# Layer 3 of a four-layer graph network: targets from node 4992 on summed from layer 0's lists, the others through 16 classes of buckets

## The chip, the cores and the metric

The kernel runs on one NeuronCore of a Trainium2 chip. A core has a matrix engine (TensorE; PE in the profile, with its weight loads shown apart as PEld), a vector engine (VectorE; DVE), a scalar engine (ScalarE; ACT), a general engine (GpSimd; POOL) and a synchronising engine (SyncE; SP) that mostly issues transfers. Sixteen DMA engines move the data. Each engine has its own instruction stream, and semaphores order the streams against each other. The metric is the device time of one execution, in microseconds (us). Ten executions of the kernel before took 8581.14 to 8597.47 us, with a median of 8588.27.

## The reference, cut to what matters

There are N = 12500 nodes of 128 features and E = 200000 edges with a source `src` and a target `dst`. The sources are uniform. The targets are the floor of 12500 times the square of a uniform number, so low node numbers have far more edges than high ones, and the edges come sorted by target. All inputs are drawn from seed 0.

```python
edge_index = stack([src, dst])
h = relu(layernorm(x)); x = x + L0(h)    # attention over the edges into dst
h = relu(layernorm(x)); x = x + L1(h)    # 8 heads, sums into row = src, reads col = dst
h = relu(layernorm(x)); x = x + L2(h)    # sums both ways, weighted by degrees
h = relu(layernorm(x)); x = x + L3(h)    # mean over the edges into dst

def L2(x):
    row, col = concat([src, dst]), concat([dst, src])
    deg = segment_sum(ones, row) + 1;  dinv = rsqrt(deg);  xw = x @ W
    return segment_sum(dinv[row] * dinv[col] * xw[col], row) + dinv**2 * xw + b

def L3(f):
    neigh = segment_sum(f[src], dst) / max(indegree, 1)
    h = f @ W_self.T + neigh @ W_neigh.T + b
    h = (h - mean(h, 0)) * rsqrt(var(h, 0) + eps) * gamma + beta   # over all nodes
    return f + relu(h)
```

## The kernel before

The nodes lie in NB = 98 blocks of P = 128, so NP = 12544 with padding. The edges lie in tiles of 128. Sums over edges are made in two ways.

**By lists and gathers.** For a tile of 128 edges a list in SBUF holds the row numbers to read, and one indirect DMA of POOL (`gather`, line 292) brings these 128 rows of a table in DRAM. A matrix of ones and zeros ("hot"), made by DVE by comparing each edge's place with a row of numbers, sums the rows into the nodes of a block by a matmul, and DVE adds the result to an accumulator in SBUF. Layer 0 works on windows of G = 4 tiles of the edges as they come, sorted by target. There are NW = 391 windows, and a window touches two blocks of targets at most; otherwise the flag `sparse`, which `windows` (line 935) makes, is set, and layer 0 sums in another way. `lists` holds a window's row numbers, places, weights of its parts (`half`), a mask for its two blocks and its first block. Layers 1 and 2 use lists by source (`sbins`), NT tiles in NG = 416 groups of four. `sum_rows` (line 1507) does layer 2's sums into the sources so.

**By buckets.** For the other direction of layer 2, and for all of layer 3, edges are cut in buckets. A bucket is one block of 128 sources and one class of targets; before, the class is the target's number modulo CLASSES = 26, and the quotient, one of COLS = 481, is its column. While layer 0 runs, the edges are sorted by a key in which source block, class, column and source lane follow each other: `pack_buckets` (line 373) makes it and `unpack_buckets` (line 388) takes it apart; both need the division by 26, which `by_class` (line 364) does in five DVE operations on the packing side. Layer 1 runs `bucket_starts` (line 749) step by step beside its own work. There are BUCKETS = 98 x 26 = 2548 buckets, held as BC = 20 columns of 128. It counts, for each bucket, how many edges come before it, gathers 128 edges from there, and stores their source lanes to `lanes` and their target columns to `places`; places of edges that belong to another bucket become -1. The start is rounded down to a multiple of STEP = 4 edges. If the 128th edge read still belongs to the bucket in any bucket, the flag `over` is set:

```python
hit = (part == head[:, c])                                 # is it this bucket's edge?
most[:m, :] = max(most[:m, :], hit[:m, P - 1:])            # the last place read
over = (ones.T @ most) > 0.5                               # at the end of bucket_starts
```

`buckets` (line 840) goes over classes four at a time (AT_ONCE), and for each four over the 98 source blocks. It loads the source block's rows (`z`) and the buckets' lanes (`lanes`), for ZB = 7 blocks with one transfer each. DVE compares the lanes of the four buckets with the lane numbers (`mine`, line 867). Then it works on pairs of buckets. For each bucket a matmul brings the sources' rows to the bucket's edges (`pout`, line 873), DVE compares the places with the column numbers (`yours`, line 875), ACT copies `pout` to `r` (line 878), and matmuls add `r` against `yours` into `sums` (line 852): features on the partitions, the class's columns along the free dimension, all 98 blocks in one accumulation. The table's rows are held as two F16 parts (PARTS = 2), so a pair makes two matmuls of 256 columns and four of 482. When four classes are through, a function `finish` takes their sums one after the other. `buckets` is a generator: it yields after each pair and each finish, so that other work can be put in between.

**Layer 2** (`layer2_edges`, from line 1566) gives the yields of `buckets` to `sum_rows`, which takes the bucket steps of its share after each of its 416 groups. Its `finish` comes from `class_rows` (line 891): it transposes the sums in pieces of up to 128 columns, copies them to `turned` (two buffers) and stores each piece to `y` in DRAM. **Layer 3** (`layer3`, from line 1644) runs `buckets` alone and puts the nodes' own part (`own_parts`: normalise, transpose, multiply by W_self, add to `yt`) in between, one step at every second yield. Its `finish` multiplies the sums by W_neigh and by the inverse degrees of the class, which `layer3_table` (line 1611) has stored by class, adds them to the class's columns of `yt`, and takes their statistics (`bst`). At the end the statistics are joined, and each group of four blocks is normalised, transposed, added to `x` and stored.

**If `over` is set**, `bucket_places` (line 830) adds -4096 to all places, so that every `yours` is zero and the buckets give zero. Both layers then sum these edges again with lists by target. Layer 2 does so in a pool named `l2a`: a loop that runs once or not at all builds the lists (`pair_lists`), and then `sum_again` (line 909) runs a loop over the NT tiles, four at each turn. Layer 3 does so in `means_again` (line 1720), ahead of its buckets: it clears an accumulator, runs `sum_again`, and multiplies the result by the inverse degrees and W_neigh. How often such a loop runs is read from a flag at run time by `count_of` (line 709). The body of a turn is written once: three loads of four tiles' lists, four gathers `rowsa`, and then, for each of the four tiles, one `hota`, two matmuls and one add.

The order of the work is that of the program text on each engine. A tile framework places the semaphores and reuses the buffers, whose number is `bufs` (one where nothing is said).

Of the kernel before, what the change touches and what calls it, by code (L numbers as in the profile page):

```python
# [69 lines left out]
CLASSES = 26  # L70
COLS = -(-N // CLASSES)
COLS2 = COLS + COLS % 2
# [34 lines left out]
class Net:  # L107
# [256 lines left out]
    def by_class(self, q, r, n):  # L364

        nc = self.nc
        nc.vector.tensor_scalar(q, n, 1.0 / CLASSES, 0.5 / CLASSES, op0=OP.mult, op1=OP.add)
        nc.vector.scalar_tensor_tensor(r, q, -float(CLASSES), n, op0=OP.mult, op1=OP.add)
        nc.vector.scalar_tensor_tensor(q, r, 0.0, q, op0=OP.is_ge, op1=OP.add)
        nc.vector.tensor_scalar(q, q, -1.0, None, op0=OP.add)  # L370
        nc.vector.scalar_tensor_tensor(r, q, -float(CLASSES), n, op0=OP.mult, op1=OP.add)

    def pack_buckets(self, key, own, other, more):
# [7 lines left out]
        self.by_class(own, more, other)  # L381
# [6 lines left out]
    def unpack_buckets(self, own, other, more, key):  # L388
# [7 lines left out]
        nc.vector.scalar_tensor_tensor(other, other, float(CLASSES), more, op0=OP.mult, op1=OP.add)  # L396
# [352 lines left out]
    def bucket_starts(self, work, take, keys, firsts, shifted, lanes, places, over):  # L749
# [6 lines left out]
        n = work.tile([P, BC], I32, name="bnum")  # L756
        nc.gpsimd.iota(n, pattern=[[P, BC]], base=0, channel_multiplier=1)
        s, k = (work.tile([P, BC], I32, name=f"b{c}") for c in "sk")
        self.by_class(s, k, n)
        nc.vector.tensor_scalar(s, s, 5, None, op0=OP.logical_shift_left)  # L760
        nc.vector.tensor_tensor(s, s, k, op=OP.bitwise_or)
# [9 lines left out]
        for h in range(5):  # L771
# [3 lines left out]
            for c in range(BC):  # L775
                below = work.tile([P, quarter], F32, name="bbelow")
                nc.vector.tensor_scalar(below, f, least[:, c:c + 1], 0.0, op0=OP.is_lt, op1=OP.add,
                                        accum_out=counts[:, c, h:h + 1])
                if c % 4 == 3:
                    yield  # L780
# [59 lines left out]
    def buckets(self, work, psum, table, lanes, place, finish):  # L840
# [14 lines left out]
        for k0 in range(0, CLASSES, AT_ONCE):  # L855
            n = min(AT_ONCE, CLASSES - k0)
            sums = [psum.tile([P, 512], F32, name=f"sums{i}", bufs=1)[:, :COLS2] for i in range(n)]
            for s in range(NB):
                if s % ZB == 0:
                    z = work.tile([P, ZB, PARTS * D], STORED, name="z", bufs=2)  # L860
                    nc.sync.dma_start(z, view[:, s:s + ZB, :])
                    lane = work.tile([P, ZB, AT_ONCE * P], F16, name="lanes", bufs=2)
                    nc.sync.dma_start(lane[:, :, :n * P], bass.AP(
                        tensor=lanes.tensor, offset=lanes.offset + (s * CLASSES + k0) * P,
                        ap=[[0, P], [CLASSES * P, ZB], [1, n * P]]))
                mine = work.tile([P, AT_ONCE * P], F16, name="mine", bufs=3)
                nc.vector.tensor_scalar(mine[:, :n * P], lane[:, s % ZB, :n * P], self.lane, None, op0=OP.is_equal)  # L867
                for i in range(0, n, 2):
                    p = psum.tile([P, 2, PARTS * D], F32, name="pout", bufs=2)
                    yours = work.tile([P, 2, COLS2], F16, name="yours", bufs=5)  # L870
                    for j in range(2):
                        b = s * CLASSES + k0 + i + j
                        nc.tensor.matmul(p[:, j, :], mine[:, (i + j) * P:(i + j + 1) * P], z[:, s % ZB, :],  # L873
                                         start=True, stop=True)
                        nc.vector.tensor_scalar(yours[:, j, :], self.iotac, place[:, b:b + 1], None,  # L875
                                                op0=OP.is_equal)
                    r = work.tile([P, 2, PARTS * D], F16, name="r", bufs=4)
# [7 lines left out]
            for i in range(n):  # L885
                o = work.tile([P, COLS2], F32, name="o", bufs=2)
# [4 lines left out]
    def class_rows(self, work, psum, out):  # L891

        nc = self.nc
        zero = work.tile([P, D], F32, name="zero")
        nc.vector.memset(zero, 0.0)
        nc.sync.dma_start(out[COLS * CLASSES:NP, :], zero[:NP - COLS * CLASSES, :])

# [746 lines left out]
    def layer3(self, keep, x, table, dbins, lanes, places, over):  # L1644
# [9 lines left out]
        with tc.tile_pool(name="l3d", bufs=1) as work, tc.tile_pool(name="ps30", bufs=1, space=PSUM) as psum:  # L1654
# [40 lines left out]
            for i, _ in enumerate(self.buckets(work, psum, ht_, lanes, place, finish)):  # L1695
                if i % 2:
                    next(parts, None)
# [259 lines left out]
```

## Time and profile before

The profiled execution took 8600.25 us. Its span, from the first to the last recorded instruction, is 8598.5 us; the granted clock of TensorE was 0.756 of full speed in the mean.

| | busy us | share of the span |
|---|---|---|
| TensorE matmuls (PE) | 6508.9 | 76% |
| TensorE weight loads (PEld) | 4581.4 | 53% |
| VectorE (DVE) | 6412.9 | 75% |
| ScalarE (ACT) | 4345.8 | 51% |
| GpSimd (POOL) | 5038.6 | 59% |

The DMA engines moved 1021.59 MB, 119 GB/s in the mean. In time order the stages are: lists and layer 0's table up to about 180 us, layer 0's edges with the sort beside them up to 2160, layer 1's table and edges up to 4600, layer 2's table up to 4858, layer 2's edges up to 7013, layer 2's output and layer 3's table up to 7160, layer 3 up to 8562, and the output up to the end. In layer 0's edges PE is busy for 1057.29 of 1980 us and POOL for 1487.22; in layer 1, from 2194 to 4600, PE is busy for 2096.63 of 2406.

How to read it: the busy time of an engine counts its own instructions. An engine can be the one that all others wait for without being busy all the time, since between two instructions there is time to issue. The rows that the prediction shows are of four kinds. A row of stages gives the stretch, its length, and each engine's busy time with its number of instructions. A row of the chain of waits gives the start, the length and what the chain went through. A row of the timeline gives the start, the length, the engine, the line and the operation, its output and inputs, and in square brackets how long the engine stood idle just ahead of it and what it waited for. A row of a group gives the least, median and longest of its instructions.

### The profile page before, as it was taken

What the parts mean: (1) busy time and instruction counts of PE and PEld (TensorE: products, weight loads), DVE (VectorE), ACT (ScalarE), POOL (GpSimd) and SP (SyncE); (2) the same over time, 40 slices, a digit from 0 to 9 for tenths busy, and PEclk for the clock granted to TensorE, in tenths of its full rate; (3) what the DMA queues carried; (4) which work ended last, traced back from release to release, by engine and by line L of the source; (5) the groups of instructions that cost most, each with busy time, mean ns of one, the idle gap of its engine ahead of it and who ended that gap; (6) DMA issues with size and microseconds to landing.
All of it is one profiled execution on the core that took longest, in us unless ns stands there. A gap on an engine that the chain in (4) does not pass through costs nothing. (4 is left out here: it accounts for less than half of the span.)

```text
span 8598.5 us, 134716 instructions
## 1 busy us (share of the span) xinstructions
PE 6508.9 (76%) x36173; PEld 4581.4 (53%) x36174; DVE 6412.9 (75%) x21784; ACT 4345.8 (51%) x8435; POOL 5038.6 (59%) x5224
## 2 busy tenths in 40 slices
PE   4455555555588898889995488888887767999998
PEld 3344544444377777778884244444444434555555
DVE  5788888887777776777777777777777776777777
ACT  4566666665455555555554333333333336555555
POOL 1777777777477777777774677777777731000000
PEclk7555555555766566665555699999999988999999
DMA  4333333334555555555553233434444443333333
GB/s 114 77 81 81 82 81 82 81 83 87 164 178 174 172 175 175 174 169 181 178 176 82 79 109 114 115 111 115 114 116 115 112 117 91 95 98 95 100 97 112
DMA packets 854249, 1021.59 MB, mean 119 GB/s; under 512 B 127765, under 2 KB 692914, under 8 KB 853232
## 3 DMA queue, kind: packets, MB, share of 16 engines
q1 hardware_dynamic: 637669, 558.29, 22.5%
q0 software_dynamic: 185728, 439.20, 18.6%
q10 hardware_dynamic: 30091, 15.25, 0.7%
q8 instruction: 319, 5.23, 0.2%
q14 instruction: 442, 3.62, 0.1%
HBM read 952.03 MB, written 60.29 MB: 118 GB/s over the span
## 5 line engine op out<-in xcount | busy, mean ns | idle before, releaser
L852 PE MATMUL sums<-yours,r 128*128 128x482 f16 x10192 | 2534.6, 373 | 219.0 <-ACT r L878 159.7
L878 ACT ACTIVATE r<-pout 128x512 f16<-128x512 f32 x2548 | 1474.0, 596 | 1948.7 <-PE pout L873 1922.7
L292 POOL DMA_INDIRECT rows<-kvt,idxs x1664 | 1621.3, 974 | 549.0 <-issue 421.2
L875 DVE TENSOR_SCALAR yours<-iotac,bucketp 128x482 f16<-128x482 f16 x5096 | 1649.1, 359 | 384.7 <-PE sums L852 384.2
L292 POOL DMA_INDIRECT rows<-zt,idxs x1664 | 1626.0, 977 | 511.2 <-issue 411.8
L292 POOL DMA_INDIRECT rows<-hw,idxd x1564 | 1489.3, 952 | 657.8 <-issue 390.1
L852 PEld LDWEIGHTS <-r 128*128 128x128 f16 x10192 | 964.8, 99 | 1036.4 <-ACT r L878 392.6
L1147 PE MATMUL psum<-rows,weights 128*128 128x130 f32 x3128 | 781.6, 422 | 589.3 <-ACT weights L1142 534.4
L1321 PE MATMUL psum<-weighted,hot 128*128 128x137 f32 x3328 | 946.1, 434 | 133.0 <-DVE acc L1323 67.6
L1147 PEld LDWEIGHTS psum<-rows,weights 128*128 128x128 f32 x3128 | 664.7, 309 | 670.2 <-ACT weights L1142 614.4
L873 PE MATMUL pout<-z,mine 128*128 128x256 f16 x5096 | 921.8, 277 | 14.3 <-DVE mine L867 9.4
L1321 PEld LDWEIGHTS psum<-weighted,hot 128*128 128x128 f32 x3328 | 733.7, 295 | 294.2 <-DVE acc L1323 195.6
L1528 DVE TENSOR_TENSOR acc<-acc,psum 128x128 f32 x1664 | 465.4, 280 | 498.4 <-PE psum L1524 492.6
L1281 ACT ACT_TABLE_LOAD x206 | 264.3, 1283 | 938.5 <-DMA near<-lengths 938.4
L873 PEld LDWEIGHTS <-mine 128*128 128x128 f16 x5096 | 479.6, 98 | 452.0 <-DVE mine L867 58.5
L1142 ACT ACTIVATE weights<-off,weight,minus 128x128 f32<-128x128 bf16 x1173 | 499.5, 482 | 383.9 <-DVE rows L1134 345.5
L1323 DVE TENSOR_TENSOR acc<-acc,psum 128x137 f32 x1664 | 487.0, 293 | 259.8 <-PE psum L1321 251.9
L1290 PE MATMUL pb<-we,near 128*128 128x8 f32 x3328 | 623.8, 325 | 3.0 <-ACT near L1281 3.0
L1290 PEld LDWEIGHTS pb<-we,near 128*128 128x128 f32 x3328 | 608.2, 281 | 20.7 <-issue 3.1
L867 DVE TENSOR_SCALAR mine<-lanes,lane 128x512 f16<-128x512 f16 (+1 forms) x1372 | 476.3, 348 | 3.1 <-PE pout L873 3.0
L1524 PE MATMUL psum<-rows,hot 128*128 128x128 f16 x3328 | 292.4, 221 | 219.1 <-DMA rows<-zt,idxs 169.3
L1316 DVE TENSOR_TENSOR weighted<-rows,weighted 128x512 f32<-128x512 f32 x416 | 271.3, 690 | 249.0 <-ACT weighted L1311 248.5
(461 smaller groups left out, 9509.2 us busy)
## 6 DMA issues: line engine op xcount, KB each, us to landing
lanes<-lanes SPq DMA_DIRECT2D x168, 896.0 KB
near<-lengths SPq DMA_DIRECT2D x208, 512.0 KB
lanes<-slanes SPq DMA_DIRECT2D x208, 256.0 KB
lanes<-dlanes SPq DMA_DIRECT2D x391, 128.0 KB
z<-zt SPq DMA_DIRECT2D x98, 448.0 KB
z<-h SPq DMA_DIRECT2D x98, 448.0 KB
rows<-kvt,idxs POOLq DMA_INDIRECT x1664
rows<-zt,idxs POOLq DMA_INDIRECT x1664
```

What stands on the lines that cost most here:

```text
L292: self.nc.gpsimd.indirect_dma_start(out=out, out_offset=None, in_=table, in_offset=bass.IndirectOffsetOnAxis(ap=idx[:, t:t + 1], axis=0))
L852: nc.tensor.matmul(sums[i], self.part(r[:, i, :], h), yours[:, i, :], start=s == 0 and h == 0, stop=s == NB - 1 and h == PARTS - 1)
L867: nc.vector.tensor_scalar(mine[:, :n * P], lane[:, s % ZB, :n * P], self.lane, None, op0=OP.is_equal)
L873: nc.tensor.matmul(p[:, j, :], mine[:, (i + j) * P:(i + j + 1) * P], z[:, s % ZB, :], start=True, stop=True)
L875: nc.vector.tensor_scalar(yours[:, j, :], self.iotac, place[:, b:b + 1], None, op0=OP.is_equal)
L878: nc.scalar.activation(r, p, AF.Copy)
L1142: nc.scalar.activation(hot[:, j, :], off, AF.Relu, bias=w[:, j:j + 1], scale=minus[:, j:j + 1])
L1147: nc.tensor.matmul(p, hot[:, j, :], rows[:, j, :n], start=j == 0, stop=j == G - 1)
L1290: nc.tensor.matmul(pb[:, j, :], hid[:, j * P:(j + 1) * P], self.we2, start=False, stop=j == W - 1)
L1321: nc.tensor.matmul(p, hot[j // G][:, j % G, :], v[:, j, :], start=True, stop=True)
L1323: nc.vector.tensor_add(d, d, p)
L1528: nc.vector.tensor_add(d, d, p[:, j, :])
```

## The change

The nodes are split at SPLIT = 39 x 128 = 4992. Targets below it form 16 classes, by their number modulo FEW = 16, of 312 columns each; targets from it on form 16 more, of 472 columns each. That makes CLASSES = 32, BUCKETS = 3136 and BC = 25. Since 16 is a power of two, shifts and masks take the place of the division, and `by_class` goes. The numbers of the buckets' keys are now the bucket numbers themselves.

Layer 2 runs all 32 classes; the number of bucket steps is 1600 in place of 1300. `class_rows` stores rows 16 nodes apart, needs no zeros behind the last class, and `turned` has one buffer.

Layer 3 runs the 16 low classes only, with z and lanes loaded for two blocks at a time (`zb` = 2, three buffers each), with fewer buffers of `mine`, `yours`, `r`, `o`, `h` and `m`, and with the inverse degrees loaded for one class at each finish. The edges of the last LATE = 146 windows of layer 0 are summed by a new function `late_sums`, from layer 0's lists, which are kept for it in DRAM (`late0` to `late3`). It runs as a generator between the bucket steps, one window at every fifth step, into an accumulator of the blocks from SPLIT / 128 - BELOW on (BELOW = 2). At its end it scales these by the inverse degrees, multiplies by W_neigh, adds them to `yt`, and takes the statistics of these columns.

A new flag `early` is set if `sparse` is, if the last edge ahead of the late windows goes to a node from 4992 on, or if `over` is. It takes the place of `over` in layer 2's `l2a`, where it decides whether the lists by target are built, and in layer 3's `means_again` and `bucket_places`; `late_sums` multiplies its masks by one minus it. `sum_again` in layer 2 still goes by `over`.

```diff
-CLASSES = 26
-COLS = -(-N // CLASSES)
+FEW = 16
+SPLIT = 39 * P
+CLASSES = 2 * FEW
+COLS = (SPLIT // FEW, (NP - SPLIT) // FEW)
+LATE = 146
+BELOW = 2
...
     def pack_buckets(self, key, own, other, more):
...
-        self.by_class(own, more, other)
+        nc.vector.tensor_scalar(own, other, int(math.log2(FEW)), None, op0=OP.logical_shift_right)
+        nc.vector.tensor_scalar(more, own, float(COLS[0]), float(FEW), op0=OP.is_ge, op1=OP.mult)
+        nc.vector.scalar_tensor_tensor(own, more, -COLS[0] / FEW, own, op0=OP.mult, op1=OP.add)
+        nc.vector.tensor_scalar(other, other, FEW - 1, None, op0=OP.bitwise_and)
+        nc.vector.tensor_tensor(more, more, other, op=OP.add)
...
     def unpack_buckets(self, own, other, more, key):
...
-        nc.vector.scalar_tensor_tensor(other, other, float(CLASSES), more, op0=OP.mult, op1=OP.add)
+        nc.vector.scalar_tensor_tensor(other, other, float(FEW), more, op0=OP.mult, op1=OP.add)
+        nc.vector.tensor_scalar(more, more, float(FEW), float(SPLIT - FEW), op0=OP.is_ge, op1=OP.mult)
+        nc.vector.tensor_tensor(other, other, more, op=OP.add)
...
-    def buckets(self, work, psum, table, lanes, place, finish):
+    def buckets(self, work, psum, table, lanes, place, finish, classes=CLASSES, zb=ZB):
...
+        n = AT_ONCE
+        for k0 in range(0, classes, n):
+            cols = COLS[k0 // FEW]
...
+                if s % zb == 0:
+                    some = 2 + (zb < ZB)
+                    z = work.tile([P, zb, PARTS * D], STORED, name="z", bufs=some)
...
+                mine = work.tile([P, AT_ONCE * P], F16, name="mine", bufs=2 + (zb == ZB))
...
+                    yours = work.tile([P, 2, COLS[classes > FEW]], F16, name="yours", bufs=4 + (zb == ZB))[:, :, :cols]
...
+                        nc.vector.tensor_scalar(yours[:, j, :], self.iotac[:, :cols], place[:, b:b + 1], None,
...
     def class_rows(self, work, psum, out):
...
-            t = work.tile([P, 4, P], F32, name="turned", bufs=2)
-            for j in range(4):
+            t = work.tile([P, 4, P], F32, name="turned")
+            part = k // FEW
+            for j in range(-(-COLS[part] // P)):
...
+                first = part * SPLIT + j * P * FEW + k % FEW
+                nc.sync.dma_start(bass.AP(tensor=out.tensor, offset=out.offset + first * D,
+                                          ap=[[FEW * D, m], [1, D]]), t[:m, j, :])
...
+        last = (NW - LATE) * G - 1
+        nc.vector.scalar_tensor_tensor(some[:, 1:2], ownf[:, last // P, P - 1:], float(SPLIT),
+                                       self.ident[:, last % P:last % P + 1], op0=OP.is_ge, op1=OP.mult)
...
+        nc.vector.tensor_copy(self.sparse, some[:, 0:1])
+        nc.vector.tensor_max(self.early, self.sparse, some[:, 1:2])
...
         with tc.tile_pool(name="l2a", bufs=1) as work, tc.tile_pool(name="ps22", bufs=1, space=PSUM) as psum:
-            once = self.count_of(work, over, 1)
+            nc.vector.tensor_max(self.early, self.early, over)
+            once = self.count_of(work, self.early, 1)
...
+    def late_sums(self, work, psum, table, lists, yt, rdeg, st):
...
+        low = SPLIT // P - BELOW
+        nc.vector.tensor_scalar(slot, slot, float(low), float(low), op0=OP.max, op1=OP.subtract)
+        fine = work.tile([P, 1], F32, name="latef")
+        nc.vector.tensor_scalar(fine, self.early, -1.0, 1.0, op0=OP.mult, op1=OP.add)
+        nc.vector.tensor_scalar(mask, mask, fine, None, op0=OP.mult)
+        acc = work.tile([P, NB - low, D], F32, name="late")
+        nc.gpsimd.memset(acc, 0.0)
+        for g in range(LATE):
+            lo = g * G
+            rows = work.tile([P, G, PARTS * D], STORED, name="rows", bufs=4)
+            for j in range(G):
+                self.gather(rows[:, j, :], table, idx, lo + j)
+            b = self.blocks_of(slot, g, 1, [DVE], NB - low - 2)
+            p = psum.tile([P, D], F32, name="psum", bufs=1)
+            for j in range(G):
+                hot = work.tile([P, P], PART, name="hot", bufs=4)
+                nc.vector.tensor_scalar(hot, self.iotac[:, :P], place[:, lo + j:lo + j + 1], None, op0=OP.is_equal)
+                for h in range(PARTS):
+                    nc.tensor.matmul(p, hot, self.part(rows[:, j, :], h), start=j == 0 and h == 0,
+                                     stop=j == G - 1 and h == PARTS - 1)
+            d = acc[:, bass.ds(b[0], 2), :]
+            for i in range(2):
+                nc.vector.scalar_tensor_tensor(d[:, i, :], p, mask[:, g, i:i + 1], d[:, i, :], op0=OP.mult, op1=OP.add)
+            yield
...
+            nc.tensor.matmul(p, self.wneigh, t[:, :k], start=True, stop=True)
...
+            nc.vector.tensor_add(v, v, p)
+            nc.vector.bn_stats(st[:, i, :], v.rearrange("p b e -> p (b e)")[:, :min(hi * P, N) - lo * P])
+            yield
...
-            self.means_again(work, psum, yt, rdeg, ht_, dbins, over)
+            self.means_again(work, psum, yt, rdeg, ht_, dbins, self.early)
...
-            place = self.bucket_places(work, places, over)
+            place = self.bucket_places(work, places, self.early)
...
             def finish(k, i, o):
...
+                rd = work.tile([P, COLS[0]], F32, name="rdegk", bufs=2)
+                nc.sync.dma_start(rd, self.rows(by_class[k:k + 1, :], COLS[0]))
...
-            for i, _ in enumerate(self.buckets(work, psum, ht_, lanes, place, finish)):
-                if i % 2:
+            sums = self.late_sums(work, psum, ht_, late, yt, rdeg, st[:, FEW:, :])
+            taken = 0
+            for i, _ in enumerate(self.buckets(work, psum, ht_, lanes, place, finish, FEW, 2)):
+                if i % 4 == 1:
                     next(parts, None)
+                while taken * 5 < i and taken < LATE:
+                    next(sums)
+                    taken += 1
+            for _ in parts:
+                pass
+            for _ in sums:
+                pass
...
+    for t, f in zip(late_lists, (lists[0][:, (NW - LATE) * G:NW * G], lists[1][:, (NW - LATE) * G:NW * G],
+                                 lists[3][:, NW - LATE:, :], lists[4][:, NW - LATE:])):
+        nc.sync.dma_start(t, f)
```

## The prediction, made before the result was known

> **What bounds the kernel now.** I read the page for the engines' shares, then the busy time by stage, since the change lies in layers 2 and 3 only. The two stages, in time order (columns: stretch, its length, busy time with instruction counts of PE, its weight loads, DVE, ACT, POOL, then granted clock, DMA share and GB/s):
>
> ```profile
> 4858.00:7013.00 2155.00, 1723.78 (x11064) 924.24 (x11064) 1583.14 (x6658) 727.19 (x1298) 1625.97 (x1664) 0.95 0.41 115
> 7160.00:8562.00 1402.00, 1382.54 (x7842) 775.15 (x7841) 1022.91 (x3332) 819.23 (x1422) 32.36 (x25) 0.99 0.33 98
> ```
>
> Layer 2 (first line) holds 1664 gathers on POOL. The chain of waits shows how they follow each other, 0.94 and 0.30 us in turn, and what one takes to land when something waits for it:
>
> ```profile
> 5248.65 0.30 issue
> 5248.96 0.94 POOL rows L292
> ...
> 5258.45 2.46 DMA rows<-zt,idxs
> ```
>
> 1664 x 1.24 is 2063 of the 2155 us, so layer 2 goes at POOL's pace; 2155 / 1664 = 1.295 us is a gather with all that interrupts it. Layer 3 (second line) has no gathers and PE is busy 1382.54 of 1402 us at clock 0.99: PE sets it. One pair of buckets there:
>
> ```profile
> 8440.49 0.98 PE L852 MATMUL sums<-yours,r 128*128 128x482 f16 x4
> 8441.31 0.38 PE L873 MATMUL pout<-z,mine 128*128 128x256 f16 x2
> 8441.52 0.98 PE L852 MATMUL sums<-yours,r 128*128 128x482 f16 x4
> ```
>
> From one row of four to the next is 1.03 us, for 4 x 482 + 2 x 256 = 2440 columns. What matters most in this case is work that is not in this execution. The lists of a bucket have 128 places, and if one bucket may not fit, flag `over` makes loops run that sum all edges again. Here `over` is 0; DVE writes the count and goes on at once past the loop:
>
> ```profile
> 7025.87 0.14 DVE L712 TENSOR_SCALAR count<-over 1x1 int32<-1x1 f32 x1 [7.92 <-DMA y<-turned]
> 7031.92 0.46 DVE L1629 MEMSET rc<- 26x482 f32 x1 [5.91 <-PE pr L1624]
> ```
>
> **Whether the new buckets fit.** This follows from the inputs, which the reference makes from seed 0, and I counted them. A bucket is one block of 128 sources and one class of targets. Its list is read from its start rounded down to a multiple of 4 (STEP), so it needs count + start mod 4, and `over` is set as soon as the 128th place read still belongs to the bucket (L804 to L810, L827). With 26 classes the largest need is 121 (count 120, start 1 past a multiple of 4): `over` is 0, as the trace shows. With the new classes one of the 3136 buckets reaches the end: sources 6528 to 6655 with targets below 4992 that are multiples of 16. It holds 125 edges (19 of them to node 0, since the targets crowd at low numbers), and 104455 edges come before it, 3 past a multiple of 4. 125 + 3 = 128: the last place read is its own last edge, and `over` becomes 1, although nothing is lost. The next largest need is 122. The other test, on the border of layer 0's lists, stays 0: the last edge ahead of the 146 late windows goes to node 4923, below 4992. But `early` takes in `over`, so both layers fall back.
>
> **The change part by part.** All sums are made on the profiled execution, 8600.25 us (span 8598.5), which is 12 above the median of 8588.27.
>
> Layer 3's buckets: 784 pairs in place of 1274, each 4 x 312 + 512 = 1760 columns, so 784 x 1.03 x 1760 / 2440 = 582 us of PE. The late edges: 146 x 4 = 584 gathers. At layer 2's 1.295 us that is 756, and the 32.4 us of POOL's adds on x come on top: 789 us, more than PE with their 146 x 8 small matmuls (0.6 us a window by layer 2's L1524 rows, 88 us). POOL sets the new stage: 789 - 1402 = -613 us. It lies between -700 (PE the bound) and -400 (every window waits for a z or lanes transfer, which now come for two blocks at a time). This holds with the flag set too: the bucket work is done on places of -4096, and its result is zero.
>
> Layer 2's buckets: 1568 pairs in place of 1274. PE: 784 pairs of 1760 columns and 784 of 4 x 472 + 512 = 2400, 582 + 794 = 1376, against 1274 x 1.03 = 1312: +64, under POOL's pace. DVE makes 98 more mine tiles (0.36 us each) and 588 more yours tiles, narrower ones, +150 of some 500 free us. Exposed is mostly `turned`, which has one buffer in place of two: each of 32 finishes on DVE waits until the 3 or 4 stores of the finish before it have landed, with the hot tiles and so PE queued behind it; seven gathered windows in advance cover a part. The chain has y<-turned for 0.4% of the span, 34 us; I take +80, from 0 to +250.
>
> Small: DVE packs with as many operations as before and unpacks with two more of 1.9 us (+4); SP issues four list stores ahead of layer 0's lanes (+3); the bucket starts have 25 columns in place of 20, spread over 104 slots of layer 1, of which 84 are used in place of 69 (+10). Together +17, from 0 to +40.
>
> The fallback, once: pair lists. In layer 1 the same items code ran from 2165 to 2194 us and its 13 chunks to 2306, beside other work: 30 + 70, and 10 to store them: 110 us (80 to 200). In layer 3 the sum is cleared (10.5 us, as the yt memset), and 25 groups each do scale, transpose, copy, matmul, add in single buffers, some 5 us each: 135 (100 to 200).
>
> The fallback's loops (L914 to L933) run NT / G = 416 turns in layer 2 and 416 in layer 3. The trace never shows one, so a turn is built from rows. All engines meet at its end, so nothing of it overlaps the next turn, and the parts add: SP issues the load of the indices, 0.38, and it lands, 2.46 as a gather's; four gathers follow, 4 x 0.94 + 3 x 0.30 = 4.66; the last lands, 2.46; two matmuls and the add, 0.5; then the meeting and the jump. The nearest rows for the last are skipped loops. Two of DVE's idle times are nothing but that (3.08 and 2.45); the third is the 5.91 above, with POOL's 2.08 in it:
>
> ```profile
> 4591.38 0.13 DVE L712 TENSOR_SCALAR count<-far 1x1 int32<-1x1 f32 x1
> 4594.60 0.23 DVE L1461 TENSOR_SCALAR eps<-eps,far 128x8 f32<-128x8 f32 x1 [3.08 <-issue]
> 4594.73 0.13 DVE L712 TENSOR_SCALAR count<-far 1x1 int32<-1x1 f32 x1
> 4597.32 0.27 DVE L1451 TENSOR_REDUCE part<-every 128x8 f32<-128x64 f32 x1 [2.45 <-issue]
> ```
> ```profile
> L1576 POOLq INC_SWDGE_SEM  x1: 2077/2077/2077, 7027.1 to 7027.1; - x1
> ```
>
> I take their mean, 3.8. A turn is 0.38 + 2.46 + 4.66 + 2.46 + 0.5 + 3.8 = 14.3 us. Low end: 2.45 for the meeting and 1.7 for each landing (estimate from edge_i, whose gather ends at 2171.37 and whose reader starts at 2173.05): 11.4. High end: 5.91 for the meeting, and 3.86 for the load (from the issue of rdegn at 7032.55 to that of rc, which waits for it, at 7036.41, with a large load between): 0.38 + 3.48 + 4.66 + 2.46 + 0.5 + 5.91 = 17.4.
>
> ```profile
> 7032.55 0.38 SPq L1627 DMA_DIRECT2D rdegn<-rt  x1
> 7032.98 0.48 SPq L1591 DMA_DIRECT2D more<-y  x1
> 7036.41 0.33 SPq L1630 DMA_DIRECT2D rc<-rdegn  x1
> ```
>
> A jump may also wait for code. After the branch of the skipped loop DVE's sequencer stands for 1.28 us between two semaphore rows:
>
> ```profile
> 7029.28 0.05 DVEq L1576
> 7029.33 1.28 issue
> 7030.61 0.05 DVEq L1576
> ```
>
> The Trainium skill, "Runtime: NRT & Kernel Launch", section Instruction fetch mechanics, says that a taken branch stalls for a fetch when its target is outside the two code pages held, of 256 instructions each. The loop is far shorter than a page on every engine, so by that rule the turns would not pay it; if each of 832 turns did pay 1.28 us, the sum would be 1065 us higher. No run shown so far has a backward jump.
>
> Sum: 8600 - 613 + 80 + 17 + 110 + 135 + 832 x 14.3 (11898) = 20227, less 12 for the median: 20215, so **20200 us**, 2.35 times the time before.
>
> **The rivals.** *The flag stays 0* (other side, faster). It decides at a single place: if that bucket held one edge fewer, or began one edge earlier, all fits. It needs other inputs than those I counted, or a test that I misread. Then the time is 8588 - 613 + 80 + 17 = 8072, 7950 to 8300. For it speaks that before's trace shows `over` 0, as counted; against it, that the same count gives 128 here.
>
> *The turns overlap* and go at the gathers' pace, 4 x 1.295 = 5.2 us: 8588 - 516 + 245 + 832 x 5.2 = 12640. Against it: every skipped loop shows all engines' semaphores waited for in sequence.
>
> *A turn costs more than its parts*: 17.4 and the 1.28 of code, 18.7: 8588 - 516 + 245 + 832 x 18.7 = 23880. For it: the gap of 1.28 us; against it: the two plain skips of 2.45 and 3.08 show none.
>
> **How the numbers follow.** Forecast (flag set, turns of 11.4 to 17.4): 0.81. Flag 0: 0.08. Overlapping turns, or any below 10.8 us: 0.04. Dearer turns: 0.07. The turn's bounds alone give 8317 + 832 x 11.4 = 17800 and 8317 + 832 x 17.4 = 22790; with the other terms' ends (-200 to +450) that is 17600 to 23240. I set 17300 to 23500. A measurement here tells 0.2% from nothing (the ten times spread by 0.2%). Faster is the flag's case, 0.08; slower is all others, 0.91; 0.01 remains for a fallback that runs in part and happens to cancel the gain.
>
> **What would show it.** Right: two long stretches of gathers named rowsa, 1664 each, one after layer 2's buckets and one ahead of layer 3's, with PE, DVE and ACT nearly idle and the clock low in them, and a period of 14 us per four gathers; between and behind them a layer 2 of some 2235 us and a layer 3 of some 790 us with POOL busy. Wrong: no rowsa at all and a time near 8070; or rowsa in one layer alone. If the stretches are there and the time is not, the size of the turn is the term to look at, its meeting first.

## The result, and the profile after

The kernel after takes 17362.99 us (median, 17345.72 to 17375.71); the kernel before took 8591.44 beside it. The ratio is 2.021, with a 95% interval of 2.019 to 2.023. The profiled execution took 17355.43 us. In two later sets of runs every kernel, the one before too, took some 20% longer, for a cause that stayed open, so times are compared only between runs beside which the kernel before took the same.

The stages of the kernel after (stretch, its length, busy time with counts of PE, weight loads, DVE, ACT and POOL, then granted clock, DMA share, GB/s):

```profile
4890.00:7640.00 2750.00, 1935.62 (x12850) 1135.60 (x12850) 1677.13 (x7373) 882.98 (x1600) 1615.55 (x1669) 0.86 0.50 100
7640.00:7700.00 60.00, 25.84 (x66) 11.84 (x66) 19.53 (x72) 4.02 (x13) 25.85 (x29) 0.50 0.14 45
7700.00:11918.00 4218.00, 617.70 (x3324) 257.82 (x3324) 918.90 (x3326) 0.00 (x0) 1569.04 (x1664) 0.50 0.11 26
...
12055.00:16267.00 4212.00, 618.07 (x3326) 228.19 (x3326) 895.28 (x3327) 0.00 (x0) 1569.20 (x1664) 0.50 0.11 26
16267.00:16388.00 121.00, 79.38 (x152) 30.46 (x152) 53.65 (x151) 1.10 (x3) 1.06 (x1) 0.50 0.01 2
16388.00:17320.00 932.00, 792.98 (x6138) 580.42 (x6138) 742.20 (x2940) 536.91 (x995) 607.26 (x610) 0.92 0.67 130
```

The third and fourth rows are the two fallback loops: 1664 gathers each, ACT idle, the clock at 0.50. The second is the building of the lists by target, the fifth the closing part of `means_again`. So the flag was set. The timeline of DVE shows it at the place where the flag is read:

```profile
7632.85 0.14 DVE L715 TENSOR_SCALAR count<-early 1x1 int32<-1x1 f32 x1 [1.69 <-DMA y<-turned]
7634.84 0.15 DVE L559 TENSOR_SCALAR low<-lane 128x1 f32<-128x1 f32 x1 [1.85 <-issue]
...
7636.36 0.13 DVE L715 TENSOR_SCALAR count<-over 1x1 int32<-1x1 f32 x1
```

Behind the count DVE goes into the code of the lists (line 559), where before went on to layer 3's table. So the direction and the stages came as forecast. But the sum has two terms that the prediction had quite otherwise. The first row, layer 2's buckets, is 2750 us long and not some 2235. And a turn of a loop is 4218 / 416 = 10.1 us, not 14.3. All of the difference, each stretch from trace to trace (before to after, profiled executions):

| stretch | before | after | difference | predicted |
|---|---|---|---|---|
| up to layer 2's first gather | 4858.7 | 4890.6 | +32 | +17 |
| from there to the last store of y | 2160 | 2741 | +580 | +80 |
| lists by target | - | 60 | +60 | +110 |
| two loops | - | 8430 | +8430 | +11898 |
| closing part of the means | - | 121 | +121 | +135 |
| the rest up to the first output (layer 2's output, layer 3) | 1554 | 1086 | -468 | -613 |
| sum | | | +8755 | +11627 |

One turn in the timeline:

```profile
8999.80 0.35 SPq L916 DMA_DIRECT2D idxa<-far  x1
...
9001.63 0.94 POOL L298 DMA_INDIRECT rowsa<-zt,idxa  x1 [5.38 <-DMA idxa<-far]
...
9005.38 0.94 POOL L298 DMA_INDIRECT rowsa<-zt,idxa  x1 [0.30 <-issue]
...
9007.97 0.37 PE L930 MATMUL psuma<-rowsa,hota 128*128 128x128 f16 x2 [0.85 <-DMA rowsa<-zt,idxa]
9008.38 0.29 DVE L933 TENSOR_TENSOR acc<-acc,psuma 128x128 f32 x1 [0.94 <-PE psuma L930]
9009.88 0.35 SPq L916 DMA_DIRECT2D idxa<-far  x1
```

Nothing of a turn overlaps the next: SP loads the indices 1.2 us after the last add has ended, and POOL waits 5.38 us for them.

### The profile page after: what moved, and what is told of

It is laid out like the page before. It is cut to its first block, busy times and chain, and to the rows that moved or that the text cites. A ratio compares the mean times of both kernels' runs of the same rounds, so it can differ in the third digit from the quotient of the medians.

```text
span 17353.7 us, 223963 instructions
## 1 busy us (share of the span) xinstructions
PE 7462.1 (43%) x43119; PEld 5125.0 (30%) x43120; DVE 8141.7 (47%) x29066; ACT 4222.5 (24%) x8327; POOL 8775.8 (51%) x9180
## 3 DMA queue, kind: packets, MB, share of 16 engines
q0 software_dynamic: 312096, 698.24, 14.3%
## 5 line engine op out<-in xcount | busy, mean ns | idle before, releaser
L930 PE MATMUL psuma<-rowsa,hota 128*128 128x128 f16 x6656 | 1236.9, 288 | 7226.1 <-DMA rowsa<-h,idxa 3620.7
L298 POOL DMA_INDIRECT rowsa<-zt,idxa x1664 | 1569.0, 943 | 2651.6 <-DMA idxa<-far 2271.2
L298 POOL DMA_INDIRECT rowsa<-h,idxa x1664 | 1569.2, 943 | 2643.5 <-DMA idxa<-far 2263.1
L930 PEld LDWEIGHTS <-hota 128*128 128x128 f16 x6656 | 486.4, 105 | 7976.6 <-DVE hota L928 3679.4
L933 DVE TENSOR_TENSOR acc<-acc,psuma 128x128 f32 x3328 | 959.6, 288 | 3814.1 <-PE psuma L930 3814.1
L928 DVE TENSOR_SCALAR hota<-iota,placea 128x128 f16<-128x128 f32 x3328 | 994.4, 320 | 2808.9 <-DMA placea<-far 2808.9
L851 PE MATMUL sums<-yours,r 128*128 128x312 f16 (+1 forms) x9408 | 1950.0, 335 | 210.2 <-ACT r L879 143.5
L879 ACT ACTIVATE r<-pout 128x512 f16<-128x512 f32 x2352 | 1335.0, 596 | 1999.2 <-PE pout L874 1964.4
L876 DVE TENSOR_SCALAR yours<-iotac,bucketp 128x312 f16<-128x312 f16 (+1 forms) x4704 | 1377.2, 327 | 57.3 <-PE sums L851 54.2
L298 POOL DMA_INDIRECT rows<-h,late x584 | 570.2, 976 | 182.3 <-issue 137.8
```

What stands on the lines that cost most here:

```text
L298: self.nc.gpsimd.indirect_dma_start(out=out, out_offset=None, in_=table, in_offset=bass.IndirectOffsetOnAxis(ap=idx[:, t:t + 1], axis=0))
L851: nc.tensor.matmul(sums[i], self.part(r[:, i, :], h), yours[:, i, :], start=s == 0 and h == 0, stop=s == NB - 1 and h == PARTS - 1)
L876: nc.vector.tensor_scalar(yours[:, j, :], self.iotac[:, :cols], place[:, b:b + 1], None, op0=OP.is_equal)
L879: nc.scalar.activation(r, p, AF.Copy)
L928: nc.vector.tensor_scalar(hot, self.iota, q[:, j:j + 1], None, op0=OP.is_equal)
L930: nc.tensor.matmul(p[:, j, :], hot, self.part(rows[:, j, :], h), start=h == 0, stop=h == PARTS - 1)
```

## Experiments

Two questions were open: whether the one full bucket sets the flag, and why layer 2's buckets became slow. A trace also records every packet of the DMA engines. In layer 2's stretch the packets of 1024 bytes, which are those of `lanes`, took 60 ns each before and 130 ns after; packets of 512 bytes (z and y) took 28 ns in both. What had changed for `lanes` is the distance between the pieces of one transfer: 26 rows of 256 bytes (6656 bytes) before, 32 rows (8192) after. My theory was that this distance slows the packets and that the gathers wait behind them. The rivals were the buffer `turned`, and an effect of the flag itself.

### n1_step2: the flag alone

```diff
-STEP = 4
+STEP = 2
```

> The kernel after with one number changed: a bucket's list starts at its first edge rounded down to a multiple of 2 instead of 4, so the fullest bucket needs 126 of 128 places. Theory (the single bucket that needed 128 set the flag): over is 0, both fallbacks are skipped, no rowsa. The time is then that of the kernel after less its fallback work: 17363 - 60 (pair lists, 7640 to 7700) - 4220 and 4212 (the two loops) - 130 (the means) + 15 (skipped loops) = 8756, since layer 2's buckets took 2716 us there and layer 3's stage 930. Rival 1 (the flag came from elsewhere, the border test or sparse): 17360 as before. Rival 2 (the slow layer 2 was an effect of the flag itself): 8070, with layer 2 at about 2235 and layer 3 at about 790 us.

Measured: 8796.93 us against 8601.04, ratio 1.023 (1.021 to 1.025). No `rowsa` is left, and DVE goes on past the loop:

```profile
7684.21 0.14 DVE L715 TENSOR_SCALAR count<-early 1x1 int32<-1x1 f32 x1 [1.71 <-DMA y<-turned]
7689.99 0.21 DVE L1596 TENSOR_SCALAR by<-dinv 128x98 f32<-128x98 f32 x1 [5.64 <-PE pr L1632]
```

The list of the full bucket now begins 1 edge ahead of it instead of 3 and ends 2 places short of the last, while no other bucket needed more than 122 of the 128 places even before this edit; so that bucket set the flag. Without it the change is still slower than before by 2.3%, 40 us more than the theory's 8756. Layer 2 is slow without the flag too, which rules rival 2 out:

```profile
4910.00:7690.00 2780.00, 1935.60 (x12849) 1134.22 (x12849) 1673.71 (x7366) 882.75 (x1600) 1608.54 (x1664) 0.86 0.52 99
...
7815.00:8762.00 947.00, 799.64 (x6139) 583.69 (x6139) 740.32 (x2942) 538.09 (x997) 612.94 (x611) 0.91 0.71 128
```

### n2_pad: lanes 33 rows apart

```diff
+ROWS = CLASSES + 1
...
-            nc.sync.dma_start(lanes[c * P:(c + 1) * P, :], lane)
+            k = P // CLASSES
+            nc.sync.dma_start(bass.AP(tensor=lanes.tensor, offset=lanes.offset + c * k * ROWS * P,
+                                      ap=[[ROWS * P, k], [P, CLASSES], [1, P]]), lane)
...
-                        tensor=lanes.tensor, offset=lanes.offset + (s * CLASSES + k0) * P,
-                        ap=[[0, P], [CLASSES * P, zb], [1, n * P]]))
+                        tensor=lanes.tensor, offset=lanes.offset + (s * ROWS + k0) * P,
+                        ap=[[0, P], [ROWS * P, zb], [1, n * P]]))
```

> As n1_step2, and the lanes of a source block stand 33 rows of 256 bytes apart in DRAM instead of 32 (8448 bytes between the blocks that one transfer reads, instead of 8192). Theory (the packets of lanes are slow because of the spacing of 8192 bytes: in the kernel after they take 130 ns of a DMA engine, in the kernel before 60 ns at a spacing of 6656): the packets go back to about 60 ns, layer 2's buckets to about 2235 us (-480), layer 3 to about 800 (-130), the whole to about 8150. Rival (the packets are slow for another reason, such as more pieces in flight or the single turned buffer): no change against n1_step2, 8756.

Measured: 8287.01 us, ratio 0.964 (0.962 to 0.965): 510 us less than n1_step2 by 256 bytes of padding. Layer 2 is where it came from (the row of stages of n2_pad):

```profile
4906.00:7200.00 2294.00, 1818.43 (x12848) 1088.89 (x12847) 1672.03 (x7363) 882.46 (x1600) 1611.24 (x1664) 0.93 0.54 119
...
7320.00:8250.00 930.00, 792.45 (x6140) 581.16 (x6141) 744.09 (x2942) 537.27 (x997) 619.15 (x611) 0.92 0.64 131
```

The theory had layer 2 right (-485 for -480), but packets only fell to 103 ns in the mean, and layer 3 gained 17 us and not 130. The median packet is back at 46 ns, that of before (96 in n1_step2); the mean is raised by the 26% of the packets that took over 100 ns (8% in before, 49% in n1_step2). POOL's waits in layer 2 show how the packets come to cost time (engine and line, what it waited for, us in total, times, longest). Before:

```profile
POOL rows L292 <- issue: 411.8, 1351, 0.3
POOL rows L292 <- DMA rows<-zt,idxs: 53.9, 177, 0.3
```

After:

```profile
POOL rows L298 <- DMA rows<-zt,idxs: 644.3, 227, 8.1
POOL rows L298 <- issue: 407.1, 1300, 6.8
```

n2_pad:

```profile
POOL rows L300 <- issue: 411.2, 1339, 2.0
POOL rows L300 <- DMA rows<-zt,idxs: 179.7, 167, 4.3
```

The 0.3 us between two gathers are the same 410 us in all three. The wait for gathered rows that land late went from 54 to 644 us by the change, and to 180 by the padding.

The records of the packets show that the rows land late, and behind what. From the end of a gather's instruction to the start of its packets it took 1.36 us before, 5.27 after and 3.18 in n2_pad, in the mean over layer 2. In the kernel after, a transfer of lanes was under way for 13 us each time (before 5). Where a gather's instruction ended within such a time, its last packet began 9.1 us later; all other gathers' last packets began after 1.8 us.

### b2_stride: the same distance in the kernel before

```diff
+ROWS = 32
...
-            nc.sync.dma_start(lanes[c * P:(c + 1) * P, :], lane)
+            a = c * P
+            while a < min(c * P + P, BUCKETS):
+                s, k = a // CLASSES, a % CLASSES
+                b = min(a + CLASSES - k, c * P + P)
+                nc.sync.dma_start(lanes[s * ROWS + k:s * ROWS + k + b - a, :], lane[a - c * P:b - c * P, :])
+                a = b
...
-                        ap=[[0, P], [CLASSES * P, ZB], [1, n * P]]))
+                        ap=[[0, P], [ROWS * P, ZB], [1, n * P]]))
```

> The kernel before, where only the place of the lanes in DRAM is changed: source blocks stand 32 rows (8192 bytes) apart instead of 26 (6656), six rows of each block being unused. Theory (spacing): lanes packets take about 130 ns instead of 60, layer 2 gets slower by 480 x 91 / 112 = 390 us, layer 3, which has no gathers and is held by PE, by less than 50; together about 8590 + 400 = 8990. Rival (spacing doesn't matter): 8590 to 8600.

Measured: 9190.68 us, ratio 1.069 (1.067 to 1.071), so +590 where 400 were expected; 523 of them are layer 2's, where 390 were expected. Packets took 137 ns. Layer 2 has the same kind of waits as after (577 us for landed rows, 644 there), and layer 3, which has no gathers and a PE at work all the time, grew by some 60 us only (waits of POOL in layer 2, then the rows of stages):

```profile
POOL rows L294 <- DMA rows<-zt,idxs: 577.0, 199, 8.7
POOL rows L294 <- issue: 422.5, 1334, 8.3
```
```profile
4863.00:7555.00 2692.00, 1836.09 (x11076) 964.64 (x11076) 1573.44 (x6670) 728.70 (x1300) 1620.54 (x1664) 0.86 0.47 92
...
7700.00:9155.00 1455.00, 1390.51 (x7821) 775.97 (x7822) 1016.09 (x3322) 810.31 (x1400) 25.11 (x20) 0.98 0.61 93
```

The DMA share of layer 3 went from 0.33 to 0.61 for the same bytes. So the distance of 8192 bytes makes the slow layer 2 by itself, without any other part of the change.

### b1_over: the fallback alone

```diff
-        nc.vector.tensor_scalar(over, p[:, 0, 0:1], 0.5, None, op0=OP.is_gt)
+        nc.vector.tensor_scalar(over, p[:, 0, 0:1], -1.0, None, op0=OP.is_gt)
```

> The kernel before with the flag over always set (the comparison is made against -1 instead of 0.5). Theory (a turn costs what its parts cost, whatever kernel it is in): two loops of 416 turns of 10.13 us each, pair lists 60 and means 130 us: 8590 + 8605 = 17195, and the turn is 10.1 us in both loops. Rival (the turn in the kernel after is cheap or dear for a reason of that kernel, such as where its code lies): a turn that differs by over 0.3 us, which is 250 us in the sum.

Measured: 17349.98 us (one run), 8749 above before. A turn is 10.27 us in both loops, 0.13 more than after, under the rival's 0.3; 832 x 0.13 = 110 is most of the 144 by which it lies above the theory's 8605. The price of the fallback hardly depends on the kernel around it: 8749 us here, and 8566 between n1_step2 and the kernel after.

### f1_eight: eight tiles a turn

```diff
-                self.sum_again(work, psum, acc, zt, dbins, over)
+                self.sum_again(work, psum, acc, zt, dbins, over, W)
```

Here `sum_again` takes the number of tiles of a turn as an argument; W is 8, and layer 3's call keeps G = 4.

> The kernel after, where one turn of layer 2's fallback loop sums 8 tiles instead of 4 (208 turns instead of 416); layer 3's loop keeps 4. Theory (a turn of 10.13 us is four gathers at 1.25 and 5.1 us of load, landing, sums and meeting that nothing overlaps): a turn of 8 is 15.1 us, the loop 208 x 15.1 = 3145 instead of 4215, the whole 17363 - 1070 = 16290; layer 3's loop stays at 10.1 a turn. Rival (the cost goes with the tiles, not with the turn): 20.2 us a turn and 17360 as before.

Measured: 18060.68 us (one run) with before at 10359.19 beside it, so the total can't be held against 16290. The loops can be read from the trace (first and last start of the gathers, in us):

```profile
L298 POOL DMA_INDIRECT rowsa<-zt,idxa x1664: 938/945/996, 9249.5 to 12417.2; - x185
L298 POOL DMA_INDIRECT rowsa<-h,idxa x1664: 938/944/962, 12562.3 to 16831.7; - x185
```

A turn of eight takes (12417.2 - 9249.5) / 208 = 15.2 us and one of four, in the same run, 10.28 (10.14 in the kernel after), so a tile costs 1.24 us, a gather's issue, and a turn 5.3 us that go with no tile. The loop became 1102 us shorter than layer 3's.

### n4_group, n5_turned, n6_tail: the rest of the excess

n4_group lays the lanes out by groups of four classes, so that the pieces of a transfer follow each other without a gap (the stores of the lanes are changed to match):

```diff
...
-                        tensor=lanes.tensor, offset=lanes.offset + (s * CLASSES + k0) * P,
-                        ap=[[0, P], [CLASSES * P, zb], [1, n * P]]))
+                        tensor=lanes.tensor, offset=lanes.offset + (k0 * BC * (P // CLASSES) + s * AT_ONCE) * P,
+                        ap=[[0, P], [AT_ONCE * P, zb], [1, n * P]]))
```

> As n1_step2, and the lanes lie in DRAM by groups of four classes, so that the blocks that one transfer reads follow each other without a gap (1024 bytes apart, where 32 rows make 8192 and 33 rows 8448). Theory (the spacing between a transfer's pieces sets what its packets take: 60 ns at 6656, 103 at 8448, 137 at 8192): packets of 1024 bytes at 60 ns or less, layer 2's buckets from 2287 in n2_pad to about 2235 us, layer 3's late gathers from 773 to about 740, the whole from 8287 to about 8200. Rival (103 ns is what the broadcast of lanes takes beside gathers, and 33 rows had already removed all that spacing does): packets at 100 ns and 8287 again.

n5_turned cuts `turned` in halves, in class_rows:

```diff
-            t = work.tile([P, 4, P], F32, name="turned")
...
+                if j % 2 == 0:
+                    t = work.tile([P, 2, P], F32, name="turned", bufs=3)
...
```

> As n4_group, and the buffer turned of class_rows is cut in halves of two pieces with three buffers, so that a finish needs not wait for the stores of the one before. Theory (the single buffer costs layer 2 part of its excess over POOL's pace): DVE's 29 us of waits for the stores go, and PE's waits for turned (112 us with its weight loads) shrink; 30 to 60 us less than n4_group. Rival (seven gathered windows in advance cover them): less than 15 us of difference.

n6_tail spreads layer 3's end:

```diff
-            p = psum.tile([P, 512], F32, name="py")[:, :k * P].rearrange("p (b e) -> p b e", e=P)
+            p = psum.tile([P, 512], F32, name=f"sums{i % 2}", bufs=1)[:, :k * P].rearrange("p (b e) -> p b e", e=P)
...
-                while taken * 5 < i and taken < LATE:
+                while taken * 27 < i * 5 and taken < LATE:
```

> As n5_turned, and layer 3's end is spread: a late window at every 5.4th step instead of every 5th, and the closing part of late_sums uses the four banks of the finished sums in turn instead of one bank for all. In n2_pad the buckets ran on for 58 us behind the last late gather and the closing part took another 72. Theory (both lie bare behind POOL's gathers): 58 to about 15 and 72 to about 45, 65 to 75 us less than n5_turned. Rival (PE is nearly as late as POOL, so that more steps per window slow the windows): only the closing part's 27 us are gained.

Measured together, with before at 10359.19: 10154.03 (0.981, 0.978 to 0.983), 10106.89 (0.975, 0.973 to 0.977) and 10043.23 (0.969, 0.967 to 0.971). The contiguous lanes come in packets of 7168 bytes at 324 ns, 46 ns for 1024 bytes; what that is worth can't be read here, since n2_pad was not beside it. The times fell by 47 us with the halves and by 64 with the spread end, about as expected. Of the 47 the traces place only 26 in layer 2 (2639 to 2613 us), where the edit acts; for the rest there is no place shown. The end, from the last store of y to the first output, fell from 1206 to 1138 us; within it the late gathers went slower (1.55 to 1.60 us each), which is the rival's point in part, and the stretch behind them fell from 152 to 59. The waits on `turned` fell by more than half with the halves. In n4_group and then in n5_turned DVE waited for the stores, and PE for the copies:

```profile
  DMA y<-turned: 7.3, 8
...
  PEld pout L906: 37.0, 32
  PE pout L906: 28.9, 24
```
```profile
  DMA y<-turned: 1.1, 2
...
  PEld pout L907: 16.3, 26
  PE pout L907: 11.5, 16
```

### m2_pad, m4_group, m6_tail, z6_tail: side by side

These are the kernels of n2_pad, n4_group and n6_tail again.

> n2_pad again, beside the next two, because the times of n4_group, n5_turned and n6_tail were taken while the chip ran every kernel some 20% slower, the kernel before too (10359 against 8601), and can't be set beside n2_pad's. Both theories: ratio to before 0.964 where before takes about 8600; where the chip is slow again, the ratio is that of this call.

> n4_group again. Theory (what lanes packets take is paid in the waits of POOL for landed gathers): with 46 ns per 1024 bytes instead of 103, layer 2's gathers go from 1.36 us a gather to about 1.31 and layer 3's from 1.326 to about 1.28; 80 + 27 = about 100 us less than m2_pad, 8190 where before takes 8600. Rival (at 103 ns the transfers were already hidden): within 20 us of m2_pad.

> n6_tail again. The halves of turned gave 47 us and the spread end 64 us while the chip was slow (10154, 10107, 10043). Theory (they are work and waits behind POOL's gathers, which a slow chip does not lengthen much): 90 to 110 us less than m4_group, about 8080, 6% below before. Rival (they were gained from idle time that only the slow chip had): less than 50 us below m4_group.

Measured, with before at 10564.87: 10345.97 (0.979, 0.975 to 0.982), 10344.37 (0.978, 0.976 to 0.981) and 10258.73 (0.970, 0.967 to 0.973). The packets of lanes fell from 98 to 45 ns for 1024 bytes with nothing gained: the rival is right here, where the gathers of both kernels went at 1.58 us, and POOL waited only 12 us in all for landed rows in m2_pad's layer 2. The last kernel gained 86 us, just under the theory's 90 to 110; the traces show 16 of them in layer 2 and 55 behind it.

> m6_tail once more, for its time where the kernel before takes about 8600. In the two calls in which every kernel was slow it was 3.1 and 3.0% faster than before, and n2_pad 2.1%; with n2_pad at 0.9637 where before took 8601. Theory (the gathers' waits for lanes, the waits for turned and the bare end of layer 3 are paid there too): 0.94 to 0.95 of before. Rival (nothing but the padding counts there): 0.964 again. If before takes over 10000 again, it tells only the repeat, 0.97.

Measured, with before at 8609.64 beside it: 8093.47 us, ratio 0.940 (0.939 to 0.941). This is the best version, 6% faster than the kernel before. Against the trace of n2_pad, layer 2 (first gather to last store) went from 2287 to 2186 us, and the time from the last late gather to the first output from 142 to 47 us. Its stages and POOL's wait in layer 2:

```profile
4890.00:7130.00 2240.00, 1801.21 (x12897) 1070.21 (x12897) 1698.01 (x7452) 885.32 (x1625) 1617.61 (x1673) 0.96 0.41 124
7260.00:8060.00 800.00, 729.08 (x6071) 557.41 (x6071) 727.99 (x2904) 525.25 (x963) 596.52 (x601) 0.99 0.57 147
```
```profile
POOL rows L298 <- DMA rows<-zt,idxs: 27.1, 87, 0.8
```

How much of layer 2's 101 us is due to the lanes and how much to the halves of `turned` was not separated beside a before of some 8600 us. The late gathers kept their 1.33 us, so the gain that n4_group's and m4_group's theories saw there did not show. Whether the lanes gave none, or the spread end took it back (it slowed these gathers in n6_tail and m6_tail), no run separates.

## Why the prediction was right, and where its terms were not

**The flag** was right, cause and place: n1_step2 frees two places in one bucket and both fallbacks vanish. The forecast's direction and most of its size follow from that count alone.

**The turn** was too dear, and it is the largest error: 14.3 us for 10.14 (means over 416 turns of layer 2's loop).

| part of a turn | predicted | measured |
|---|---|---|
| load of the indices, issue to the first gather | 0.38 + 2.46 | 1.88 |
| four gathers | 4.66 | 4.69 |
| the last one's landing, sums and add | 2.46 + 0.5 | 2.36 |
| meeting and jump | 3.8 | 1.21 |

The step that failed is "I take their mean, 3.8": a skipped loop's 2.45 to 5.91 us were taken for a turn's meeting and jump. In before's gap of 2.45 us DVE's sequencer first reads the count (0.31 us for the load), and after the branch it passes twelve rows of semaphores, 1.2 us in all. In the kernel after each engine reads counts 8 times in the whole execution, so no turn does, and from a turn's last add to the next load it is 1.21 us. The landings were taken at 2.46, from the chain of waits; in the turn shown above the last one is 1.65, the 1.7 of the low end. The additive form itself held: f1_eight finds 5.3 us beside the gathers. A turn below 10.8 us was given 0.04, together with turns that overlap; 10.14 is below it, and yet nothing overlaps. All turns together make -3470 us.

**Layer 2's buckets** were the second error, +580 for +80, beyond the +250 of the range's end. The step "PE: +64, under POOL's pace ... Exposed is mostly `turned`" looked at engines and buffers only. It didn't ask what 32 classes do to the addresses that a transfer of lanes reads. n2_pad, b2_stride and POOL's waits show it. Whether the foreseen +80 is a part of it is not shown: POOL's waits for landed rows alone grew by 590 us. With the lanes padded layer 2 is 127 us longer than before, and these waits 126; in z6_tail, with `turned` in halves, it is 26 us longer, with waits 27 us shorter.

The Trainium skill, "DMA: Bandwidth & Descriptors", section Latency and other measured facts, has a row on HBM row pitch at large powers of two: rates halve at a pitch of 4 MiB, and one should pad by a few KiB or lay out contiguously. Its pitches are from 512 KiB up. Here it shows at 8 KiB already, in a transfer where all partitions read the same seven pieces: 137 ns for 1024 bytes in the mean, 103 with 256 bytes of padding, 60 at 6656, 46 without a gap. The mechanism behind it, on the memory's side, no run here shows.

**Layer 3** was -468 for -613. POOL did set it, and its pace was right: the late gathers took 781 us where 789 were reckoned for POOL. Left out was the end: behind the last late gather come the last buckets and the closing part of `late_sums`, 150 us up to the first output (142 in n2_pad, 47 in z6_tail).

**The small terms**: lists 60 for 110, means 121 for 135, the start +32 for +17 (about +50 in n1_step2 and n2_pad).

So 17363 lies in the range, close to its low end, but that is luck: errors of both signs met, and the turns' -3470 alone would have made 16750, below 17300. **The rival that the flag stays 0** was wrong in its time as well: 8072 was forecast, to 8300 at most, and n1_step2 took 8797, on the slower side of before. Only the padding brings it to 8287.

The Trainium skill, "Runtime: NRT & Kernel Launch", section Instruction fetch mechanics, was cited for a loop shorter than a code page, which should not wait for code. The trace agrees: add to next load takes 1.21 us in all in the mean, so on this path the turns did not pay the 1.28 us seen after the skipped loop.

## What to carry to other kernels

Where a limit is tested, count what the inputs need against it for every new way of cutting them: here 1 of 3136 buckets cost 8.6 ms. When the number of parts becomes a power of two, look at the distances it gives to transfers (here 8192 bytes; no other power of two was measured), and give pieces that one transfer reads a place side by side. Price a loop's turn from its own chain of load, issue, landing and meeting, and not from skipped loops, which also read their counts and pass other waits.

## What the runs showed of the hardware that was not expected

Slow packets of one queue cost time through another's: DVE waited 0.7 us in all for lanes in the kernel after's layer 2, and it was the gathers, whose own packets of 4096 bytes took no longer (219 ns before, 202 after, in the mean), that landed late behind them. POOL's waits for them in layer 2 rise with the time for 1024 bytes of lanes, in the runs beside a before of some 8600 us: 27 us at 48 ns in z6_tail, 54 at 60, 180 at 103, 644 at 130 in the kernel after, and 577 at 137 in the kernel before with 8192 bytes.
